# Moving small products, factor sums and a router's preparation in a decoder kernel's attention steps

## The chip, the cores and the metric

The kernel runs on one core of a Trainium2 chip. The metric is the device time of one execution in microseconds (us). The time of the kernel before is the median of three runs.

## The reference

The program is a chain of four layers over tokens of 512 features, each a condition block and a feed-forward block with a residual: `x = x + ffn(cond(x))`. The change touches the third layer (attention, then a feed-forward block with a small router). Cut to what matters:

```python
# attention: 8 sequences x 128 new tokens, 32 query heads, 8 key heads, 512 cached positions
q = rope(rmsnorm(x @ Wq.T));  k = rope(rmsnorm(x @ Wk.T));  v = x @ Wv.T
kc, vc = k_cache[block_table], v_cache[block_table]
k_all, v_all = concat(kc, k), concat(vc, v)            # 640 positions, each key head for 4 query heads
probs = softmax(where(valid, q @ k_all.T * SCALE, -1e30))
cond = (probs @ v_all) @ Wo.T
# feed-forward of the same layer, fed with cond
H = cond @ W.T + b;  z = cond @ A
logits = 0.5 * H[anchors, :8] / scale_H + 0.5 * (z[anchors] @ LiMEs.T) / scale_z
weights = soft_top2(softmax(logits)), repeated for 2 tokens
x = x + H + (z * (weights @ LiMEs)) @ Bmat * scaling
```

Everything is float32. Each step of the chain is computed in full by both kernels.

## The kernel before, in words

The kernel keeps all tokens in on-chip memory. The first two layers come first; then `attention(...)` works in 32 **steps** (`steps`, one for each pair of a group of four query heads with its key head, `qd` of 0 to 7, and a pair of sequences, `p` of 0 to 3). Step n is `qd = n // 4`, `p = n % 4`. In a step there are two halves, j = 0 and 1, one for each sequence of the pair.

The order of the work is written out by hand in `run`: what passes through `kept(...)` stays in program order on its engine. Instructions without it are placed by a scheduler.

What a step n does, with the functions and lines to follow in the code:

- `weigh(n, j)` (L1118, L1122): five score products `st` on TensorE (PE), each followed by an exponential on ScalarE (ACT) into `pT`. `added(n, j)` (L1138): four additions on VectorE (DVE) sum the five blocks of `pT` into `part`.
- `summed(n, j)` (L1146): four small products with ones on PE sum `part` over the partitions. `inverted` (L1153): the reciprocal on DVE. `spread` (L1159, L1161): four copies on DVE and three transfers on the queue of SyncE (SP) give `R` for all partitions; a fourth transfer stores the sums.
- `mix(n, j)` (L1169): five products with the values. `divided` (L1179): `oT` = product times `R`.
- `project(n + 1)`: queries, keys and values of the next step, as seven block products in place of eight (`seven`, L959). The products, in order, are called one, p6 (tile `q_six`), p5 (tile `q_five`), six (tile `q_six` too), and then the second parts of one, p5 and six. Between them stand DVE's additions `u1` (L972), `u2` (L974) and the results (L1008), ACT's copies, and the hooks of the dictionary `at`, which put other work between the products: a hook "c22" runs after the results of the fourth product have been queued.
- `leave(n - 1)`: the output projection of the step before, by the same `seven`, with tiles `wo_one`, `wo_two`, `wo_six`. GpSimd (POOL) makes two of its additions into `y` (L1207, L1202).
- `rotate`, `roots`, `rotated`, `normed`, `turn` prepare the new queries and keys: POOL multiplies by the sines (L1048), DVE by the cosines (L1052: queries' term 128x1024, keys' term 128x256), adds, scales and turns blocks of 32x32 (L1097). SP writes them to memory (`turned_new`, L1090), and `fetch` reads them back in another order (`qT` L1106, `kTn` L1108). Cached keys go the same way (`turn_cached`, L1081, L1086).
- `gather` (L904): POOL collects cached keys and values, eight gathers each.
- `seven` needs sums and differences of its operands' blocks. Those of the tokens are `tokens` (L920), those of the weights `factors()` (L868): four DVE operations for Wq, Wk and Wv of a `qd`, four for Wo. The weights' factors are needed once for each `qd`: those of Wq in the step before its first projection, those of Wo in the step after the first.

`ending(...)` (L1654) holds the feed-forward block of this layer and the fourth layer. It loads six small tensors at once (`small`, L1676, and two more), and clears and loads `b16` (L1690, L1691). Its `prepare` (L1696) turns `A2` with four PE transposes, copies it, multiplies it with `LiT` in four products and copies the result into `WH`. `end.shifted` (L1748) adds a bias to `x` on POOL. In step 30 and 31, `end.turn`, `end.low`, `end.anchors` and `end.product` start the feed-forward block.

On-chip accumulator tiles come from three tags: `st` (three buffers: scores, p6 and the small sums), `mm` (three: one, p5 and six of both projections), `av` (two).

Before the loop, `first(0)` and `first(1)` project and turn steps 0 and 1 while the second layer ends.

## Time and profile before

| what | us |
| --- | --- |
| median of three runs | 1609.87 (1606.64 to 1612.54) |
| the profiled execution | 1615.59 |
| its span, first to last instruction | 1613.7 |
| PE busy / share of the span | 1543.0 / 96% |
| DVE busy | 1078.4 / 67% |
| POOL busy | 850.3 / 53% |
| ACT busy | 537.9 / 33% |
| mean granted TensorE clock | 0.987 |

A row of the profile's timeline gives the start of an instruction (or of several alike, merged), how long it took, the engine (PEld is PE's loading of weights, SPq an issue of SP's queue), the line, the operation, output tile and input tiles, sizes, and in brackets how long the engine stood idle before it and what ended that wait. A row of the waits gives who waited for whom, the total in us, how often, and the longest. A transfer's row is its issue; it lands later.

The steps start, in the profiled execution, where the first `st` product of a step starts: step 0 at 344.75, step 1 at 374.38, step 2 at 407.73, step 31 at 1420.17. Most steps take 33.5 to 35.3 us.

### The profile page before, as it was taken

To read this page: it belongs to the slowest core of one execution; us is meant where nothing else is said; L and a number is where in the kernel's file an instruction comes from. 1 tells how busy PE (TensorE), PEld (TensorE's weight loads), DVE (VectorE), ACT (ScalarE), POOL (GpSimd) and SP (SyncE) were. 2 spreads that over 40 slices of the span, in tenths; PEclk is the share of its full clock that TensorE was granted. 3 is DMA by queue.
4 is the path that set the end of the run, shared out by engine and by line. 5 is a ranking of instruction groups with operands and counts; after the bars stand their busy time and mean duration, and the time that the engine had idled before them with its cause. 6 is when DMAs were issued, how large, how long until landed. Compare 5 with 4: busy or idle time off the path is not lost.

```text
span 1613.7 us, 18969 instructions
## 1 busy us (share of the span) xinstructions
PE 1543.0 (96%) x5985; PEld 925.5 (57%) x5985; DVE 1078.4 (67%) x2123; ACT 537.9 (33%) x1324; POOL 850.3 (53%) x842
## 2 busy tenths in 40 slices
PE   9999998959999999999999999999999999989998
PEld 7888884525555555555555555555555544559653
DVE  4575423466878887787878778777777888843141
ACT  1111110234443444344543434543444444320210
POOL 1341106173766777776777766777757677700000
PEclk9999999979999999999999999999999999999999
DMA  8110003043546444553454444355444435512000
GB/s 293 40 47 24 1 0 98 27 118 83 163 111 185 119 124 120 146 167 102 123 152 122 121 139 139 98 144 158 119 137 114 120 98 144 151 39 71 0 20 35
DMA packets 161358, 169.92 MB, mean 105 GB/s; under 512 B 55713, under 2 KB 128609, under 8 KB 161121
## 3 DMA queue, kind: packets, MB, share of 16 engines
q1 hardware_dynamic: 143104, 131.61, 28.7%
q0 software_dynamic: 17056, 36.49, 7.7%
q8 instruction: 50, 0.82, 0.2%
q10 hardware_dynamic: 1088, 0.52, 0.1%
q14 instruction: 60, 0.48, 0.1%
HBM read 113.89 MB, written 42.07 MB: 97 GB/s over the span
## 4 chain that ended last, share of the span: by engine, by line
PE 70%; DVE 12%; issue 7%; POOL 4%; DMA 4%; SPq 2%; ACT 1%; DVEq 0%; ACTq 0%; POOLq 0%
PE st L1118 11%; PE av L1169 11%; PE g L362 7%; PE q_six L959 5%; PE q_five L959 5%; PE dn L362 4%; PE wo_two L959 4%; DVE part L1138 3%; PE q_one L959 3%; PE wo_six L959 3%; PE wo_one L959 2%; PE z L53 2%; PE h L1672 2%; POOL kn L904 2%; PE o L53 2%
## 5 line engine op out<-in xcount | busy, mean ns | idle before, releaser
L904 POOL DMA_INDIRECT kn<-in_k_cache,kvrow_k x256 | 294.0, 1149 | 75.8 <-issue 67.9
L904 POOL DMA_INDIRECT vals<-in_v_cache,kvrow_v x256 | 261.1, 1020 | 73.6 <-issue 68.6
L1169 PE MATMUL av<-pT,vals 128*128 128x512 f32 x640 | 298.8, 597 | 0.0
L1122 ACT ACTIVATE pT<-st,hide 128x512 f32<-128x512 f32 x256 | 176.0, 688 | 346.4 <-PE av L1169 146.3
L1118 PE MATMUL st<-qT,kT 128*128 128x512 f32 x512 | 241.8, 606 | 10.3 <-DMA qT<-turned_new 8.3
L1048 POOL TENSOR_TENSOR vq<-q,txq 128x256 f32<-128x256 f32 x128 | 120.4, 969 | 198.9 <-ACT sqq L1032 134.9
L1169 PEld LDWEIGHTS av<-pT,vals 128*128 128x128 f32 x640 | 119.1, 190 | 144.5 <-issue 137.8
L1118 PEld LDWEIGHTS st<-qT,kT 128*128 128x128 f32 x512 | 99.0, 194 | 121.7 <-issue 116.1
L1138 DVE TENSOR_TENSOR part<-pT 128x512 f32<-128x512 f32 x128 | 87.4, 685 | 39.9 <-issue 23.7
L1179 DVE TENSOR_TENSOR oT<-av,R 128x512 f32<-128x512 f32 x64 | 44.2, 691 | 85.4 <-DMA R<-R 34.7
L959 PE MATMUL q_one<-q,x 128*128 128x384 f32 x256 | 93.0, 486 | 0.0
L1159 DVE COPY R<-rr 32x128 f32<-32x128 f32 x256 | 84.8, 331 | 3.7
L1032 ACT ACTIVATE sqq<-q 128x128 f32<-128x128 f32 x256 | 79.4, 310 | 11.1 <-DVE q L1008 4.2
L1153 DVE RECIPROCAL rr<-sum 128x128 f32<-128x128 f32 x64 | 60.9, 952 | 23.5 <-PE q_five L959 21.0
L1013 ACT COPY q<-q_one 128x256 f32<-128x256 f32 x32 | 11.9, 372 | 187.4 <-PE q_one L959 180.2
L959 PEld LDWEIGHTS q_one<-q,x 128*128 128x128 f32 x256 | 48.5, 190 | 39.8 <-issue 14.5
L959 PE MATMUL q_six<-q_s,xs_all 128*128 128x384 f32 x192 | 70.0, 487 | 0.0
L959 PE MATMUL wo_one<-o,oT 128*128 128x256 f32 x256 | 65.8, 379 | 0.0
L1118 PE MATMUL st<-qT,kTn 128*128 128x512 f32 x128 | 65.4, 592 | 0.0
L1207 POOL TENSOR_TENSOR y<-y,uo 128x512 f32<-128x512 f32 x32 | 40.9, 1277 | 45.4 <-DVE y L1199 44.9
L959 PE MATMUL wo_two<-o_s,os 128*128 128x256 f32 x256 | 60.5, 379 | 0.0
L362 PE MATMUL g<-xs,ws 128*128 128x256 f32 (+1 forms) x240 | 55.2, 379 | 1.5 <-POOL ws L429 1.5
(394 smaller groups left out, 2729.4 us busy)
## 6 DMA issues: line engine op xcount, KB each, us to landing
turned_new<-qkt SPq DMA_DIRECT2D x128, 160.0 KB
turned_cached<-kt SPq DMA_DIRECT2D x128, 128.0 KB
kT<-turned_cached SPq DMA_DIRECT2D x32, 512.0 KB
qT<-turned_new SPq DMA_DIRECT2D x32, 512.0 KB
R<-R SPq DMA_DIRECT2D x192, 64.0 KB
q<-in_WqT SPq DMA_DIRECT2D x8, 1024.0 KB
o<-in_WoT SPq DMA_DIRECT2D x8, 1024.0 KB
kn<-in_k_cache,kvrow_k POOLq DMA_INDIRECT x256
```

The source lines that it names most:

```text
L53: pe.matmul(o, lhsT, rhs, start=start, stop=stop)
L362: pe.matmul(o, lhsT, rhs, start=start, stop=stop, skip_group_check=True)
L904: kept(pool.indirect_dma_start(out=d[:, c, :], out_offset=None, in_=kc if what == "k" else vc, in_offset=bass.IndirectOffsetOnAxis(ap=kvro ...
L959: kept(pe.matmul(o, l[:, c, :], r[:, c, :], start=start and c == 0, stop=c == 1, skip_group_check=True))
L1032: kept(act.activation(sq, S[n][m][:, j, i, :], AF.Square, accum_out=S[n]["ssq"][:, j, col : col + 1]))
L1048: kept(pool.tensor_tensor(to, t[:, b, :, hi : hi + 64], wx[:, b, lo : lo + 64].unsqueeze(2).to_broadcast(list(to.shape)), ALU.mult,))
L1118: kept(pe.matmul(ps, s["kT"][:, c, 4 * j : 4 * j + 4, :] if c < 4 else s["kn"][:, j], s["qT"][:, :, REP * j : REP * (j + 1), :].rearrange( ...
L1122: kept(act.activation(pT[:, c, :, :].rearrange("p i t -> p (i t)"), ps, AF.Exp, **(dict(bias=hide[:, b, c : c + 1]) if c < 4 else dict(bia ...
L1138: kept(dve.tensor_tensor(o, l, r, ALU.add))
L1153: kept(dve.reciprocal(r, S[n]["sum", j]))
L1159: kept(dve.tensor_copy(R[0:32, i * P : (i + 1) * P], r[32 * i : 32 * i + 32, :]))
L1169: kept(pe.matmul(ps, v[:, c, :], pT[:, c, :, :].rearrange("p i t -> p (i t)"), start=c == 0, stop=c == NC - 1, skip_group_check=True,))
```

## The change

No arithmetic is added or taken away. Work is put elsewhere:

- **Products with ones of the first half.** In the steps that project a next one (1 to 30), `summed(n, 0)`, with `inverted` and `spread`, moves from behind the projection's second product to behind its fourth (hook "c22"). The second half of the output's differences (`outs`) moves behind `u2`.
- **Factors.** Of Wq's four factors, two stay at the end of the step that starts them (n % 4 == 2), one goes among the next step's sums of `pT`, one to hook "u2". Wo's four are spread over "u2", "c22", "c12" and the output projection's "u2". Wo's first factors move from before step 0 into step 1.
- **The keys' cosine term.** `rotate` now returns it as a function, and it is queued behind `u2` of the output projection.
- **The ending.** `ending` is built at the end of step 4 in place of before step 0, with its loads and its memset kept in program order. `prepare` becomes a generator of two parts: the transposes and the first copy come behind the second products with ones of step 5, the products and the copy into `WH` behind that step's last products with the values.
- **Step 0.** Its first products with ones, `fetch(1)`, reciprocal and spread come behind the sums of the second half; `tokens(2)` comes behind the sums of the first half; `divided(0, 0)` comes behind both reciprocals.
- The gather of values of the next step is called before the loads of the ending in step 30. In the order that results, POOL's two additions into `y` stand ahead of that gather in step 30; in all other steps they already did.

```diff
-        end = ending(
-            tc, a, out, x, ident, bias3, experts, late,
...
-        y2 = att.run(late, end, bank, lambda: sp.dma_start(kept, x))
+        def end_of(in_order):
+            return ending(
+                tc, a, out, x, ident, bias3, experts, late,
...
+        y2, end = att.run(late, end_of, bank, lambda: sp.dma_start(kept, x))
@@ rotate
-            kept(dve.tensor_tensor(r, t, ws.unsqueeze(2).to_broadcast(full), ALU.mult))
-            return r, u
+            def straight_terms():
+                kept(dve.tensor_tensor(r, t, ws.unsqueeze(2).to_broadcast(full), ALU.mult))
+
+            S[n]["r" + m] = r, u
+            return straight_terms
...
+        terms("q", S[n]["q"], REP)()
+        return terms("k", S[n]["k"], 1)
@@ run
-        end.prepare(bank)
-        tokens(2)
-        every(WO[0].factors())
-        wo_ops = iter(())
+        end, prepared = None, iter(())
+        w_ops, wo_ops = iter(()), WO[0].factors()
...
             some(outs, 2)()
+            some(w_ops)()
             every(sums_of)
             if after:
                 project(after, {
-                    "six": lambda: summed(n, 0),
-                    "u1": lambda: (some(wo_ops)(), every(outs), inverted(n, 0)),
-                    "u2": lambda: (spread(n, 0), some(wo_ops)()),
+                    "u2": lambda: (every(outs), every(w_ops), some(wo_ops)()),
+                    "c22": lambda: (summed(n, 0), inverted(n, 0), spread(n, 0), some(wo_ops)()),
                     "c11": lambda: (squares(after, "k", 0, (0,)), squares(after, "q", 0, (0, 1))),
-                    "c12": lambda: squares(after, "q", 0, (2, 3)),
+                    "c12": lambda: (squares(after, "q", 0, (2, 3)), some(wo_ops)()),
                 })
-                some(wo_ops)()
-                rotate(after)
+                keys_terms = rotate(after)
...
-                    "u2": lambda: every(wo_ops),
+                    "u2": lambda: (keys_terms(), every(wo_ops)),
...
                 fetch(after)
-            else:
+                gather(after, "v")
+            elif n:
                 summed(n, 0)
                 every(outs)
                 inverted(n, 0)
                 spread(n, 0)
-                if n:
-                    leave(n - 1)
-                else:
-                    fetch(1)
-            if after:
-                if n + 2 == len(steps):
-                    end.load_w2()
-                    end.load_aw()
-                    end.shifted()
-                gather(after, "v")
+                leave(n - 1)
+            else:
+                tokens(2)
+            if n + 2 == len(steps):
+                end.load_w2()
+                end.load_aw()
+                end.shifted()
             mixed = mix(n, 0)
             weigh(n, 1, {2: (some(mixed),), 3: (some(mixed),), 4: (some(mixed, NC),)})
             every(added(n, 1))
-            divided(n, 0)
+            if n == 0:
+                summed(n, 0)
+                fetch(1)
+                inverted(n, 0)
+                spread(n, 0)
+            else:
+                divided(n, 0)
             summed(n, 1)
             inverted(n, 1)
             spread(n, 1)
+            if n == 0:
+                divided(n, 0)
+            if n == 5:
+                prepared = end.prepare(bank, lambda shape, name: wk.tile(shape, F32, tag="xs", name=name, bufs=1))
+            next(prepared, None)
             every(mix(n, 1))
+            next(prepared, None)
...
-                        every(W[steps[n + 2][0]].factors())
+                        w_ops = W[steps[n + 2][0]].factors()
+                        some(w_ops, 2)()
                     tokens(n + 2)
             if n == 3:
                 kept(keep())
+            if n == 4:
+                end = end_of(kept)
@@ ending
-        sp.dma_start(t, src)
+        kept(sp.dma_start(t, src))
...
-    sp.dma_start(WH[:, :, 0:8], chunks(a["W2T"])[:, :, 0:8])
+    kept(sp.dma_start(WH[:, :, 0:8], chunks(a["W2T"])[:, :, 0:8]))
     b16 = early.tile([P, 16], F32, tag="b16", name="b16")
-    pool.memset(b16, 0.0)
-    sp.dma_start(b16[:, 0:8], a["b8"].partition_broadcast(P))
+    kept(pool.memset(b16, 0.0))
+    kept(sp.dma_start(b16[:, 0:8], a["b8"].partition_broadcast(P)))
...
-    def prepare(bank):
+    def prepare(bank, room):
+
         pt = bank("mm", [P, D], "A2Tp")
         for c in range(DC):
-            pe.transpose(pt[:32, c * P : (c + 1) * P], A2[:, c, :], ident)
-        A2T = early.tile([32, D], F32, tag="oT", name="A2T")
-        act.copy(A2T, pt[:32])
+            kept(pe.transpose(pt[:32, c * P : (c + 1) * P], A2[:, c, :], ident))
+        A2T = room([32, D], "A2T")
+        kept(act.copy(A2T, pt[:32]))
+        yield
         ps = bank("mm", [P, DC, 8], "alp")
         for c in range(DC):
-            mm(ps[:, c, :], A2T[:, c * P : (c + 1) * P], LiT, True, True)
-        act.copy(WH[:, :, 8:16], ps)
+            kept(pe.matmul(ps[:, c, :], A2T[:, c * P : (c + 1) * P], LiT, start=True, stop=True))
+        kept(act.copy(WH[:, :, 8:16], ps))
```

## The prediction

> **What bounds the kernel now.** I read first the busy times by engine, and then what TensorE (PE) waited for, longest first.
>
> ```profile
> PE 1543.0 (96%) x5985; PEld 925.5 (57%) x5985; DVE 1078.4 (67%) x2123; ACT 537.9 (33%) x1324; POOL 850.3 (53%) x842
> ...
> PE sum L1146 <- DVE part L1138: 21.2, 19, 5.5
> PE wo_two L959 <- DVE uo L974: 8.5, 9, 2.1
> PE st L1118 <- DMA qT<-turned_new: 8.3, 1, 8.3
> ...
> PE st L1118 <- DMA R<-R: 2.0, 1, 2.0
> ```
>
> PE is busy for 96% of the span, and the change takes no matmul away. All that can be won is PE's idle time, and the slowed matmuls that follow a long idle. Nearly all of it lies in the attention's 32 steps, and the waits name what ends it: the products with ones (L1146) wait for VectorE's sums. So I cut PE's timeline where each step's first score product starts. These are the stretches of steps 0, 3, 4, 7, 13, 28 and 30 (length, then busy time of each engine, then granted clock):
>
> ```profile
> 344.75:374.38 29.63, 23.10 (x56) 9.63 (x57) 16.36 (x30) 6.76 (x10) 15.41 (x15) 0.82 0.48 127
> 441.36:478.80 37.44, 35.06 (x113) 19.18 (x112) 30.21 (x56) 15.06 (x37) 24.16 (x25) 0.95 0.38 102
> 478.80:512.49 33.69, 33.55 (x113) 18.25 (x112) 26.65 (x52) 15.05 (x37) 23.90 (x25) 1.00 0.58 176
> 580.88:615.16 34.28, 33.41 (x113) 18.39 (x112) 28.67 (x52) 15.07 (x37) 24.48 (x25) 1.00 0.41 112
> 785.44:820.70 35.26, 34.02 (x113) 18.11 (x112) 27.91 (x52) 15.05 (x37) 24.97 (x25) 1.00 0.48 139
> 1304.27:1340.37 36.10, 33.67 (x113) 18.29 (x112) 29.87 (x50) 15.05 (x37) 26.62 (x25) 1.00 0.39 106
> 1377.56:1420.17 42.61, 38.49 (x171) 22.18 (x169) 30.96 (x52) 16.23 (x39) 25.39 (x23) 1.00 0.48 141
> ```
>
> Step 1, which waits for nothing, takes 33.35 us with the same 113 groups: that is PE's own time. VectorE is busy 27 to 30 us of such a step, so it can pass as long as its order suits. All times below are counted from a step's start.
>
> **Steps 1 to 31: the products with ones.** Before, they stand behind the projection's second product (PE is there at 7.1 us), and VectorE ends the last sum of pT at 7.14 at best. After, they stand behind the fourth, at 9.5. The wait is then covered for sums up to 2.3 us late. I sum by kinds of step.
>
> Even steps 2, 4 to 26 (13 of them): 437.95 us together, to 33.35 each, -4.4. Steps 7, 11, 15, 19, 23: VectorE makes four factors of Wq (0.95 each) at the end of the step before, and the sums come 0.9 late. After, two of the four lie there and two among the sums; parts end at 8.0 and cover holds. 171.4 to 166.8, -4.7. Steps 3 and 27 have token combinations besides (four of 0.42), and the wait is 2.4 to 2.9, after which PE runs slow:
>
> ```profile
> 450.77 0.47 PE L1146 MATMUL sum<-part,ones 128*32 128x128 f32 x8 [2.38 <-DVE part L1138]
> 451.17 2.93 PE L959 MATMUL q_five<-q_s,xs_all 128*128 128x384 f32 x4
> ```
>
> After, oT starts at 3.4 in place of 5.1 and the sums are ready by 8.7: 75.3 to 67.0, -8.3.
>
> Steps 9, 13, 17, 21 make the four factors of Wo (0.69 each, 1.25 beside a GpSimd product). They lose at three places: sum, q_six, and wo_two, which waits for the add L974 behind the two rotary terms. After, u2's add no longer stands behind the reciprocal, and k's term (0.95) is moved behind L974. Adding the starts of the queue's instructions in the new order from 7.14, I get L974 done at 17.9, where PE wants it at 18.2. But VectorE's work is the same, so the turned queries (L1097) come at 22.4 in place of 23.1 to 23.7. From there to the next step's first product pass 11.3 us in the mean (write, fetch, completion; from 10.7 to 11.9 by step), and these steps have 0 to 0.8 us of slack there now: the queries' fetch becomes the bound, at 33.9. 140.9 to 135.6, -5.3. Step 25 is of this kind (36.22 to 34.1, -2.1), step 29 too, with its sums 1.1 later (37.19 to 34.5, -2.7). Step 1 becomes such a step, since Wo's first factors move into it: 33.35 to 33.95, +0.6. Step 5 gets the ending's router: four transposes (0.60) and eight small products (1.05) on PE, less what overlaps: 34.71 to 34.8, +0.1. Its second part (the copy into WH) is 0.19 on ScalarE in step 6's beginning, where ScalarE has 7.6 us idle. The six loads move on SP's queue to step 5, between kT (9.8) and R (12.8): 6 x 0.42 = 2.5, which just fits; the memset of 0.13 lies in GpSimd's gap.
>
> **Steps 28 and 30: a stall that only shrinks.**
>
> ```profile
> 1319.41 4.58 POOL L1748 TENSOR_TENSOR x<-x,bcol 128x2048 f32<-128x2048 f32 x1
> ...
> 1320.45 3.82 DVE L1052 TENSOR_TENSOR r<-k,tsk 128x256 f32<-128x256 f32 x1
> 1324.19 0.41 DVE L972 TENSOR_TENSOR uo<-wo_two,uo 128x256 f32<-128x256 f32 x1
> ```
>
> k's term takes 3.82 in place of 0.95 and PE waits 2.1 behind it. By the rows alone, moving it behind the adds frees PE: -2.7 at step 28. The Trainium skill (SBUF — State Buffer, Who interferes with whom) speaks against that: a VectorE instruction with two SBUF inputs and a GpSimd one that reads SBUF exclude each other for the whole instruction, whichever came second waits; with one input from PSUM there is no clash. The trace agrees: the adds from PSUM take 0.42 beside GpSimd. So k's term still waits for the end of GpSimd's addition, now at 19.3, and y's first add stands behind it, which the last product (wanted at 19.1) waits for until 20.2. Step 28 goes to 34.8, -1.3, and I take that; step 30 likewise, -1.1. In 30 GpSimd's two additions into y move ahead of the gather of values, away from the copies of R (L1159 took 2.00 there instead of 0.22). SP issues the last queries' fetch behind two transfers of R, so it goes out about 2 us sooner, and with the idle of 2.16 goes the half clock at step 31's head. Of some 5 I take -4.5 for 30 and 31, because y's additions now meet the sums of pT.
>
> **Step 0: the fetch of the first queries.**
>
> ```profile
> 328.45 1.50 DVE L1097 STREAM_TRANSPOSE qkt<-r 128x1280 f32<-128x1280 f32 x1
> ...
> 334.99 0.13 POOL L1690 MEMSET b<- 128x16 f32 x1
> ...
> 335.15 0.34 SPq L1691 DMA_DIRECT2D b<-in_b  x1
> 335.60 1.95 SPq L1090 DMA_DIRECT2D turned_new<-qkt  x4
> ...
> 340.24 0.65 SPq L1106 DMA_DIRECT2D qT<-turned_new  x1
> 344.75 5.60 PE L1118 MATMUL st<-qT,kT 128*128 128x512 f32 x8 [8.31 <-DMA qT<-turned_new]
> ```
>
> The turned queries are there at 329.95, but SP writes them at 335.60: its queue stands at the load of b, which waits for a memset behind GpSimd's gathers. With the ending moved, the write goes out at 330.0, the fetch at 334.6 (4.64 later, as now), the first product at 339.2 (4.51 later). Then PE has 40 records of 0.43 = 17.2, 0.7 of products with ones, 2.1 of half clock at the start as now, and one wait: it is at the second products with ones at 354.6. VectorE's queue sets their inputs: L1097 of step 1 ends at 349.8 (it waits for a landing that the change leaves alone), then four sums, four token combinations (1.45) and four sums (2.8 each four): 356.9, so 2.3 idle. Step 1 starts at 361.7. A rule makes it later: the clock falls after an idle window, and the windows of about 3.4 us run free (the Trainium skill, TensorE: Matmul & The Clock Gate, What's actually happening). The rows cannot say for 2.3: 2.38 idle was followed by half clock in step 3, 2.11 in step 28 was not. The rows alone give 361.7, the rule up to 363.4; I take 362.9 against 374.4, -11.5. Step 1's own fetch, now ahead of R, lands at about 359.5 and is covered.
>
> **The sum**, on the profiled execution (1615.59, of it 1613.7 span): -11.5 +0.6 -4.4 -4.7 -8.3 -5.3 +0.1 -2.1 -2.7 -1.3 -4.5 = -44.1. The stalls set at nothing can only come out above it, so I take -42: 1573.6 for such an execution. The profiled one lies 5.7 above the median, so the median is 1609.87 - 42 = 1568.
>
> **Rivals.**
> *The reciprocal waits for a late completion.* In step 4 it starts 2.77 us after the products with ones and only "until q_five"; in step 7 after 1.00. Sixteen even and Wo steps show the long form. If it keeps it behind the fourth product, the reciprocal starts at 12.2 in place of 10.3, and the rest of the queue, the queries' fetch included, slides by 1 to 1.7: even steps +0.15, Wq steps +0.2, seven Wo steps +1.5. Sum +14: 1580. For it: the two steps with no wait before these products, 25 and 30, show it. Against: in step 1, with none either, and at all second halves but one it is prompt.
> *Step 0 gives little.* If the earlier write crosses the gathers of keys (GpSimd issues them until 335) or PE then stands longer at the sums, its gain is 3 to 5: 1575.
> *GpSimd's addition overtakes.* In step 28 the query term started 0.14 us before it. If it starts after, it is blocked for 3.5 and PE for about 3, twice, and the clock falls: +9, 1577.
> *The change doesn't do what it says: the late queue goes on to the next wait.* If VectorE is the true limit of all steps, the waits reappear at wo_two and at the fetch, and only step 0, 3, 27, 30 and 31 gain: 1586.
> *Slower.* Everything from the reciprocal on is moved behind the fourth product's two adds. If that brings the turned queries later than 23.5 in even and Wq steps (21.3 now; slack in the fetch 0.7 less the 0.3 that the step is shorter), each of 28 steps pays beyond that. From 1.6 us per step on it takes all back; at 2, 1620. Nothing shows 2.2 us of such delay: the late completion accounts for 0.9.
>
> **How the numbers follow.** As summed 0.51; late completion 0.24; step 0 small 0.08; overtaking 0.05; VectorE's limit 0.06; slower 0.04; no change 0.02. About 0.3% (5 us) is what a measurement can tell from none. Ends of the unknown: step 0 at best -12.7, Wo steps at 33.5, 28 and 30 as the rows alone have them, in all -53: 1556. Late completion with half of step 0 lost, -44 +14 +6: 1586. So 1556 to 1588; the likeliest case alone 1558 to 1576. Faster 0.94, same 0.02, slower 0.04.
>
> **What would show it.** SP's write of turned_new at about 330 and the first score product near 339; no wait of sum on part except in steps 0 and 31; even steps of 33.35; wo_two's wait on uo small, a new one of wo_six on y in 28 and 30; Wo steps at 33.9 with st waiting for qT. Wrong if the reciprocal idles until q_five's end, if wo_two waits for q_five's bank, or if L1097 starts after 22.5 in even steps.

## The result, and the profile after

The median went from 1611.2 us (four runs, 1606.6 to 1616.5) to 1589.7 (four runs, 1588.6 to 1592.5): 0.9868 of the time before, 95% interval 0.9834 to 0.9902, or 21.5 us. The forecast was 1568, with 1556 to 1588. The sign was right, the size half of what was forecast, and the result lies 1.7 us outside the range. The profiled executions went from 1615.6 to 1588.6, 27.0 us. One run among all of the study was slow, over 1.5% above the fastest of its kernel (the profiled one of `b_undo_factors2`, 1609.9); it is left out of the medians below and not read.

The busy times of the kernel after, and what its TensorE waited for (total, times, longest):

```profile
PE 1536.3 (97%) x5985; PEld 925.2 (58%) x5985; DVE 1088.0 (69%) x2123; ACT 537.8 (34%) x1324; POOL 849.9 (54%) x842
```

```profile
PE sum L1152 <- DVE part L1144: 9.1, 4, 5.1
...
PE wo_six L962 <- DVE y L1205: 5.2, 10, 0.8
PE st L1124 <- DMA kTn<-turned_new: 4.9, 1, 4.9
...
PE st L1124 <- DMA qT<-turned_new: 2.0, 3, 1.2
...
PE hd L53 <- issue: 1.0, 1, 1.0
...
PE wo_two L962 <- DVE vals L1011: 0.7, 1, 0.7
```

The wait of the products with ones (`sum`, now L1152) fell from 21.2 us in 19 places to 9.1 in 4, as the change set out to do. Two things are new: the last output product `wo_six` waits in ten steps for `y` (L1205), and 5.1 us of the rest stand in one place, step 0. The same stretches as before (steps 0, 3, 4, 7, 13, 28, 30), in the kernel after:

```profile
339.49:368.01 28.52, 23.40 (x56) 9.83 (x57) 17.54 (x31) 6.87 (x10) 17.88 (x18) 0.78 0.50 133
435.29:469.89 34.60, 33.99 (x113) 18.06 (x112) 30.72 (x55) 14.95 (x37) 23.96 (x24) 1.00 0.41 111
469.89:503.31 33.42, 33.42 (x112) 18.47 (x113) 26.89 (x53) 15.06 (x37) 23.99 (x26) 1.00 0.58 177
572.13:605.48 33.35, 33.35 (x113) 18.30 (x112) 28.82 (x50) 14.96 (x37) 23.07 (x24) 1.00 0.42 115
773.46:807.45 33.99, 33.61 (x114) 18.31 (x113) 27.58 (x49) 15.06 (x37) 23.18 (x23) 1.00 0.50 141
1279.15:1315.12 35.97, 33.85 (x114) 18.12 (x112) 27.96 (x53) 15.05 (x37) 28.65 (x26) 1.00 0.42 109
1350.09:1392.50 42.41, 38.57 (x170) 22.14 (x169) 29.47 (x53) 16.23 (x39) 26.87 (x24) 1.00 0.50 145
```

Steps 3, 4 and 7 came down to about the floor of 33.35. Steps 28 and 30 hardly moved, and step 0 got 1.1 us shorter where 6 were forecast. Every step cut in this way gives the account below. The last column is an execution of the same changed kernel in the last group of runs (group 5 of the experiments).

| part | before | forecast | after | after, last group |
| --- | --- | --- | --- | --- |
| first product of step 0 | 344.8 | 339.2 | 339.5 | 340.5 |
| start of step 1 | 374.4 | 362.9 | 368.0 | 365.5 |
| step 1 | 33.35 | 33.95 | 33.94 | 33.93 |
| 13 even steps | 438.0 | 433.6 | 433.8 | 433.6 |
| steps 7, 11, 15, 19, 23 | 171.4 | 166.8 | 166.7 | 166.7 |
| steps 3 + 27 | 75.3 | 67.0 | 68.9 | 66.7 |
| steps 9, 13, 17, 21 | 140.9 | 135.6 | 137.3 | 135.8 |
| step 5 | 34.7 | 34.8 | 35.4 | 35.4 |
| steps 25 + 29 | 73.4 | 68.6 | 70.1 | 68.9 |
| step 28 | 36.1 | 34.8 | 36.0 | 36.1 |
| step 30 to the end | 236.2 | 231.7 | 236.7 | 233.4 |
| span | 1613.7 | 1569.6 | 1586.7 | 1575.9 |

Against the sum of -44.1, 17.1 us are missing: 5.1 up to step 1, 5.0 from step 30 on, 1.9 in steps 3 and 27, 1.7 in the four Wo steps, 1.5 in 25 and 29, 1.2 in 28, and the rest in small amounts.

**Step 0.** VectorE and TensorE of the kernel after (in brackets the idle time ahead and what ended it; `remote` is an end that the profile could not trace to an instruction):

```profile
352.71 0.69 DVE L1144 TENSOR_TENSOR part<-part,pT 128x512 f32<-128x512 f32 x1
...
354.45 0.42 DVE L923 TENSOR_TENSOR xs<-x,xs 128x256 f32<-128x256 f32 x1
358.08 1.29 DVE L1144 TENSOR_TENSOR part<-pT 128x512 f32<-128x512 f32 x2 [3.21 <-remote]
...
355.40 0.43 PE L1152 MATMUL sum<-part,ones 128*32 128x128 f32 x8
360.95 0.65 PE L1152 MATMUL sum<-part,ones 128*32 128x128 f32 x8 [5.12 <-DVE part L1144]
```

The forecast let VectorE go from the token combinations (`xs`, done at 354.87) straight to the second half's sums. It stands idle for 3.21 us instead. `part` has one buffer in the program, and the second half may not be written into it until the first products with ones have read it. Those were moved behind the last of the first half's products with the values and run at 355.40 to 355.83. VectorE starts only at 358.08, which is 2.2 us later still: it saw the end of the products late. Such **late ends** come back below.

**Steps 28 and 30.** GpSimd (POOL), VectorE and TensorE in step 28, and then in step 30:

```profile
1293.90 4.58 POOL L1766 TENSOR_TENSOR x<-x,bcol 128x2048 f32<-128x2048 f32 x1
...
1296.68 2.08 DVE L1056 TENSOR_TENSOR r<-k,tsk 128x256 f32<-128x256 f32 x1
1298.69 0.41 DVE L1205 TENSOR_TENSOR y<-wo_six,y 128x256 f32<-128x256 f32 x1
1300.07 1.46 DVE L1068 TENSOR_TENSOR r<-r,vq 128x1024 f32<-128x1024 f32 x1 [0.97 <-POOL vq L1051]
...
1315.12 1.13 PE L1124 MATMUL st<-qT,kT 128*128 128x512 f32 x2 [1.23 <-DMA qT<-turned_new]
...
1377.23 1.65 POOL L1213 TENSOR_TENSOR y<-y,uo 128x512 f32<-128x512 f32 x1 [4.44 <-DVE y L1205]
1377.07 2.35 DVE L1144 TENSOR_TENSOR part<-pT 128x512 f32<-128x512 f32 x2
1381.41 0.43 PE L1152 MATMUL sum<-part,ones 128*32 128x128 f32 x8 [1.59 <-DVE part L1144]
```

The keys' term (L1056) ends with GpSimd's addition, as forecast from the Trainium skill (SBUF — State Buffer, Who interferes with whom): 1298.76 against 1298.48, 2.08 us in place of 0.95. What the forecast left out stands one row on: two of GpSimd's own four products `vq` are queued behind the same addition, so the rotated queries come late (0.97 idle), and the next step's first score waits 1.23 for their fetch. In step 30 the two additions into `y`, moved ahead of the gathers, fall on the sums of pT: two sums take 2.35 in place of 1.27 (step 28), and the second products with ones wait 1.59.

### The profile page after: what moved, and what is told of

It is laid out like the page before. It is cut to its first block, busy times and chain, and to the rows that moved or that the text cites. A ratio compares the mean times of both kernels' runs of the same rounds, so it can differ in the third digit from the quotient of the medians.

```text
span 1586.7 us, 18970 instructions
## 1 busy us (share of the span) xinstructions
PE 1536.3 (97%) x5985; PEld 925.2 (58%) x5985; DVE 1088.0 (69%) x2123; ACT 537.8 (34%) x1324; POOL 849.9 (54%) x842
## 4 chain that ended last, share of the span: by engine, by line
PE 83%; DVE 6%; POOL 4%; DMA 3%; issue 3%; ACT 1%; SPq 1%; another core or an unknown queue 0%; ACTq 0%; DVEq 0%; POOLq 0%
PE st L1124 16%; PE av L1175 16%; PE g L362 7%; PE q_six L962 7%; PE q_one L962 5%; PE q_five L962 5%; PE dn L362 5%; PE wo_two L962 4%; PE wo_six L962 3%; PE wo_one L962 3%; PE z L53 2%; PE h L1688 2%; PE o L53 2%; PE sum L1152 2%; PE eo_l L53 1%
## 5 line engine op out<-in xcount | busy, mean ns | idle before, releaser
L907 POOL DMA_INDIRECT kn<-in_k_cache,kvrow_k x256 | 280.6, 1096 | 75.7 <-issue 66.9
L907 POOL DMA_INDIRECT vals<-in_v_cache,kvrow_v x256 | 255.2, 997 | 73.6 <-issue 57.8
L1051 POOL TENSOR_TENSOR vq<-q,txq 128x256 f32<-128x256 f32 x128 | 125.5, 1010 | 173.2 <-DVE q L1011 156.7
L1165 DVE COPY R<-rr 32x128 f32<-32x128 f32 x256 | 104.5, 408 | 4.7
L962 PE MATMUL q_one<-q,x 128*128 128x384 f32 x256 | 96.2, 498 | 0.0
L1128 ACT ACTIVATE pT<-st,rs 128x512 f32<-128x512 f32 x64 | 44.0, 687 | 38.4 <-PE st L1124 20.4
```

The source lines that it names most:

```text
L907: kept(pool.indirect_dma_start(out=d[:, c, :], out_offset=None, in_=kc if what == "k" else vc, in_offset=bass.IndirectOffsetOnAxis(ap=kvro ...
L962: kept(pe.matmul(o, l[:, c, :], r[:, c, :], start=start and c == 0, stop=c == 1, skip_group_check=True))
L1051: kept(pool.tensor_tensor(to, t[:, b, :, hi : hi + 64], wx[:, b, lo : lo + 64].unsqueeze(2).to_broadcast(list(to.shape)), ALU.mult,))
L1128: kept(act.activation(pT[:, c, :, :].rearrange("p i t -> p (i t)"), ps, AF.Exp, **(dict(bias=hide[:, b, c : c + 1]) if c < 4 else dict(bia ...
L1165: kept(dve.tensor_copy(R[0:32, i * P : (i + 1) * P], r[32 * i : 32 * i + 32, :]))
```

## The experiments

The kernels were run in five groups. The kernels of a group ran side by side on one chip, with runs of the kernel before among them, so times are given as ratios to those. Medians of different groups are not to be compared directly. "After" is the changed kernel; `after_again`, `after_third`, `after_fourth` and `after_fifth` are the same kernel run again.

| group (before) | kernel | median us | ratio, 95% interval |
| --- | --- | --- | --- |
| 1 (1607.1) | a_sums: sums moved alone | 1586.0 | 0.9868 [0.9836, 0.9900] |
| 1 | a_ending: ending moved alone | 1608.4 | 1.0006 [0.9991, 1.0020] |
| 1 | b_undo_sums: after, sums back | 1590.1 | 0.9887 [0.9855, 0.9920] |
| 1 | b_undo_factors: after, factors back | 1577.6 | 0.9828 [0.9786, 0.9870] |
| 2 (1610.1) | after_again | 1587.8 | 0.9866 [0.9848, 0.9883] |
| 2 | before_again (one run) | 1617.5 | |
| 2 | c_step0 (one run) | 1592.6 | |
| 2 | c_all | 1581.6 | 0.9815 [0.9798, 0.9833] |
| 3 (1613.7) | after_third | 1595.1 | 0.9896 [0.9872, 0.9920] |
| 3 | b_undo_factors2 | 1593.6 | 0.9877 [0.9844, 0.9909] |
| 3 | c_keys_shift | 1585.1 | 0.9827 [0.9804, 0.9850] |
| 3 | c_all2 | 1583.2 | 0.9819 [0.9795, 0.9842] |
| 4 (1608.1) | after_fourth | 1589.3 | 0.9878 [0.9852, 0.9903] |
| 4 | after_gather | 1586.5 | 0.9860 [0.9839, 0.9881] |
| 4 | c_gather | 1578.4 | 0.9812 [0.9790, 0.9835] |
| 5 (1605.6) | after_fifth | 1577.8 | 0.9818 [0.9793, 0.9843] |
| 5 | a_sums2: sums moved alone | 1586.5 | 0.9872 [0.9849, 0.9896] |

### One part of the change alone

`a_sums` is the kernel before with only the first half's products with ones moved:

```diff
-                    "six": lambda: summed(n, 0),
-                    "u1": lambda: (some(wo_ops)(), every(outs), inverted(n, 0)),
-                    "u2": lambda: (spread(n, 0), some(wo_ops)()),
+                    "u1": lambda: some(wo_ops)(),
+                    "u2": lambda: (every(outs), some(wo_ops)()),
+                    "c22": lambda: (summed(n, 0), inverted(n, 0), spread(n, 0)),
```

> The kernel before with one part of the change alone: the first half's products with ones, reciprocal and spread behind the projection's fourth product, the output's differences behind u2. Theory (the sums are late by less than two products take): the wait of sum on part goes from steps 2 to 29; the even steps come to 33.35 us (-4.4 together), steps 7, 11, 15, 19, 23 to 33.4 (-4.7), steps 3 and 27 to 34.5 (-6), steps 9, 13, 17, 21 hardly change (35.0, their wait goes on to wo_two), step 0 keeps its 29.6 and its start at 344.7; in all -15 to -17. Rival (VectorE's queue is the limit and its lateness goes on to the next wait): the Wq steps and steps 3 and 27 keep two thirds of their loss as waits of q_six and wo_two; in all -7.

Measured: even steps 433.6 together, the five Wq steps 166.7, steps 3 + 27 66.7, the four Wo steps 136.8 (137.5 in `a_ending` beside it, which has the order of before in them); step 0 starts at 342.8 and takes 27.6. The theory holds and was too careful: 21 us by the medians. This one edit makes the even steps, the Wq steps and steps 3 and 27 (with the token combinations) what they are after the change.

`a_ending` is the kernel before with only `ending` built behind step 4 and prepared in step 5.

> The kernel before with the ending alone built behind step 4 and prepared in step 5; the order of step 0 and everything else as before. Theory A (what the prediction assumed: step 0's start carries through to step 1's): first score product at 339.5 in place of 344.75 and step 1 starts 5 us or more sooner, at 369 or below. Theory B (VectorE's queue, which stands until 348 to 349 at the turning of step 1's queries, sets the first half's sums): the first score product comes at 339.5 all the same, but the first products with ones stay at 356.7 and step 1 starts at 373.5 to 374.5; gain 0 to 1 us in all.

Measured: ratio 1.0006, the first score product at 339.83, step 1 at 373.20. Theory B. TensorE and VectorE in step 0 of this kernel:

```profile
339.83 1.70 PE L1121 MATMUL st<-qT,kT 128*128 128x512 f32 x3 [3.83 <-DMA kTn<-turned_new]
...
353.68 0.68 DVE L871 TENSOR_TENSOR o_s<-o,o_s 128x512 f32<-128x512 f32 x1
...
357.28 0.65 PE L1149 MATMUL sum<-part,ones 128*32 128x128 f32 x8 [11.22 <-DVE part L1141]
```

Five microseconds were won at the start of step 0 and nearly all were lost at the next wait, which grew from 5.5 to 11.2: VectorE goes through the turned queries, the token combinations and four factors before it reaches the sums. So the sooner fetch is worth nothing by the median without the new order of step 0 behind it.

### One part of the change undone

`b_undo_sums` puts the first half's products with ones back behind the second product, and `b_undo_factors` puts the weights' factors back where they stood (second diff):

```diff
+                    "six": lambda: summed(n, 0),
+                    "u1": lambda: (every(outs), inverted(n, 0)),
-                    "u2": lambda: (every(outs), every(w_ops), some(wo_ops)()),
+                    "u2": lambda: (every(w_ops), spread(n, 0), some(wo_ops)()),
-                    "c22": lambda: (summed(n, 0), inverted(n, 0), spread(n, 0), some(wo_ops)()),
+                    "c22": lambda: some(wo_ops)(),
```

```diff
-            some(w_ops)()
-                    "u2": lambda: (every(outs), every(w_ops), some(wo_ops)()),
-                    "c22": lambda: (summed(n, 0), inverted(n, 0), spread(n, 0), some(wo_ops)()),
+                    "u1": some(wo_ops),
+                    "u2": lambda: (every(outs), some(wo_ops)()),
+                    "c22": lambda: (summed(n, 0), inverted(n, 0), spread(n, 0)),
-                    "c12": lambda: (squares(after, "q", 0, (2, 3)), some(wo_ops)()),
+                    "c12": lambda: squares(after, "q", 0, (2, 3)),
-                        some(w_ops, 2)()
+                        every(W[steps[n + 2][0]].factors())
```

> The changed kernel with the first half's products with ones back behind the projection's second product, the reciprocal at u1 and the spread at u2, the factors still spread. Theory: the wait of sum on part returns in the even steps (33.7 each, +4.4), in 7, 11, 15, 19, 23 (34.3 each, +4.7) and in 3 and 27 (+5), in all +14 to +17 over the changed kernel. Rival (the spread factors alone would have freed VectorE in time): +5.

> The changed kernel with the weights' factors where they stood before: Wq's four at the end of the step, Wo's at u1, u2, behind the projection and at the output projection's u2. Theory (cover of two products, 2.3 us): the Wq steps stay at 33.4 (their sums come 0.9 late, which is covered), steps 3 and 27 lose 1 each, the Wo steps stay within 0.5 of 34.3; in all +1 to +4. Rival (the spreading is what made room): waits of sum on part return in 7, 11, 15, 19, 23 with 0.5 or more, in all +8.

Measured: `b_undo_sums` lies 12.5 us above its neighbour `b_undo_factors`, by the ratios 9.5. The loss does not lie where either side put it: the even steps take 445.8 in place of 433.6 (+12.2; +4.4 was expected), the Wq steps 167.8 (+1.0; 34.3 each was expected), steps 3 + 27 69.5 (+2.8; +5 was expected), and the Wo steps are shorter, 134.4. So the moved sums count most in the even steps. In the Wq steps and in 3 and 27 the change without them still does much of what they do alone: in the order of before (`a_ending`, same group) these take 171.6 and 73.6. Without the moved sums the kernel is still 17.0 us below the kernel before, so the gains of the parts do not add up.

With the factors put back, all Wq steps stay at 33.35 and the Wo steps at 33.94. The median, 1577.6, was 12 us below the 1589.7 of the changed kernel, where 1 to 4 above (or 8 above, by the rival) was expected. That comparison was between groups, and the next ones showed that it misleads.

### The same kernels once more, side by side

> The kernel before once more, profiled beside the other experiments. Theory (the execution shown first was a slow one of its kind): the span comes out near the run with the ending alone, whose steps have the same order (1604 to 1609), with steps 3 and 27 together at 73.6 (75.3 in the execution shown) and steps 9, 13, 17, 21 at 137.5 (140.9). Rival: it repeats 75.3 and 140.9, and the ending's move is what shortened them.

Measured, in one run: span 1615.7, the Wo steps 141.0 again, as the rival has it; steps 3 + 27 at 73.3, as the theory has it. So the profiled execution of before shown first was no accident; but in group 1 the same order of steps (`a_ending`) had given 137.5.

> The changed kernel once more, profiled and timed beside the other experiments. Theory (the spread factors themselves cost time): steps 9, 13, 17, 21 again at 136.5 to 137.5 and steps 3 and 27 at 68.5 or more, where the kernel with the factors put back has 135.8 and 66.7; median 1584 to 1590, slower than that kernel's 1577.6. Rival (the execution shown was unlucky): it reads like the kernel with the factors put back, 1576 to 1580.

Measured: 1587.8, Wo steps 137.1, steps 3 + 27 67.6 (68.5 or more was expected). It reads like the result shown first. That the spread factors are the reason is not shown by this; the next pair tests it.

> The changed kernel a third time, as the first rung of a ladder whose four kernels are run side by side: changed kernel, factors put back, two more edits in the steps, step 0 mended. Theory: about 22 us under the kernel before (ratio 0.986 to 0.988), step 0 at 25 to 29 and steps 9, 13, 17, 21 at 135 to 137.

> The changed kernel with the weights' factors put back where they stood, beside the changed kernel. Theory (the earlier gap of 10 us between the two is mostly that they were not run side by side; step by step the factors' spreading costs 0.5 in steps 9 to 21, 0.7 to 2 in 3 and 27): 2 to 4 us under the changed kernel. Rival (spreading costs what the medians said): 8 us or more under it. Second rival (spreading helps, as it was costed at -5.3 with its cover): above the changed kernel.

Measured: 1595.1, with a step 0 of 32.0 and Wo steps of 138.6, both above what was expected; and 1593.6 for `b_undo_factors2`, whose runs spread from 1583.9 to 1598.7. The difference of 1.5 us is below the theory's 2 to 4 and small against that spread: no worth of the factors' spreading can be told either way. So the 10 us between groups 1 and 2 was not the factors. It is a difference between groups, and the profile shows one: how long VectorE's reciprocal stands idle for the products with ones. Kernel before, kernel after (both as shown first), and `a_sums2` of group 5:

```profile
DVE rr L1153 <- PE q_five L959: 21.0, 16, 1.6
```

```profile
DVE rr L1159 <- PE sum L1152: 2.5, 9, 0.5
```

```profile
DVE rr L1153 <- PE sum L1146: 0.9, 1, 0.9
```

In groups 1 and 5 this idle time is at most 0.9 us in the whole execution of every kernel, the order of before (`a_ending`) included. In the executions shown first and in groups 2 to 4 it is 2 to 18, and 20 to 23 in the order of before. In the execution of before shown first the reciprocal stands idle 1.5 to 1.6 us in each of twelve steps, with the products with ones over; in the changed kernel mostly 0.3 to 0.5 in a step, and longer in step 0. It is not the chip alone: by the record groups 4 and 5 ran on the same chip (number 2), about nine minutes apart.

### Mending step 0

`c_step0` starts from the kernel with the factors put back; the second half's sums of step 0 get a tile of their own, and the token combinations go behind them:

```diff
+        if (n, j) == (0, 1):
+            both = late[0].tile([P, 4, 2, P], F32, tag="os", name="parts_0_1").rearrange("p a b t -> p (a b t)")
+            t, u = both[:, 0 : REP * P], both[:, REP * P :]
...
-            else:
-                tokens(2)
...
             if n == 0:
+                tokens(2)
                 summed(n, 0)
```

> The changed kernel with the factors put back where they stood, and step 0 mended: the sums of its second half go into a tile of their own, and the four token combinations come behind them. Theory (the second products with ones wait because VectorE may not write the second half's sums until the first half's products have read the buffer): their wait of 3.2 us or more falls to 0.5 or less, and the half clock behind it goes; step 0 takes 20.5 to 22.0 in place of 25.2. Rival (VectorE's queue behind the turned queries is late by itself): the wait stays above 2, step 0 above 24.

Measured: step 0 takes 20.84, as the theory says: the shared buffer made most of the wait (the edit also takes the four token combinations, 1.45 us by the prediction, from ahead of these sums). But step 1 took 41.7 in place of 33.9. TensorE stops 1.9 us into it for 4.8 us. By the trace it is released there by the second reciprocal, which comes 10 us behind the products that it reads and holds a bank that the scores need.

`c_all` adds two edits, which `c_keys_shift` below has alone, and `c_all2` gives step 0's products with ones a bank that the scores do not use:

```diff
-        S[n]["sum", j] = ps = psa.tile([P, P], F32, tag="st", name=f"sum_{n}_{j}", bufs=3)
+        S[n]["sum", j] = ps = psa.tile([P, P], F32, tag="st" if n else "mm", name=f"sum_{n}_{j}", bufs=3)
```

> As the kernel with step 0 mended, and two edits more: the keys' cosine term behind the output projection's first result in place of ahead of it, and the bias of the ending added to x on ScalarE in step 31 (eight operations) in place of GpSimd in steps 28 and 30. Theory: the wait of wo_six on y goes everywhere (0.5 in steps 1, 5, 9, 13, 17, 21, 25, 29 and 0.95 in 28 and 30), step 28 comes to 33.4 (36.1), step 30 to 39 (40.8), the Wo steps to 33.4; 1562 to 1566. Rival (the queries' fetch is the bound behind it): the Wo steps keep 33.8 with a wait of st for qT, and step 30 keeps its wait of sum; 1570 to 1573.

> As the third rung, with step 0 mended: its second half's sums in a tile of their own, the token combinations behind them, and step 0's products with ones in a bank that the scores do not use. Theory A (the stall in step 1 came from the score's bank, held until the second reciprocal): step 0 at 20.8 and step 1 at 33.4, 7 us under the third rung. Theory B (TensorE's results are seen late there whatever the bank): step 0 at 20.8, step 1 at 38 or more, within 2 us of the third rung.

Measured: `c_all` 20.7 and 40.4 for steps 0 and 1, `c_all2` 21.0 and 41.0. By the medians, 1581.6 and 1583.2. Both expectations for `c_all` miss (1562 to 1566, 1570 to 1573): step 28 comes to 33.35 and step 30 to 39.7, but step 1 stays at 40.4, and the four Wo steps take 139.1. `c_all2` lies 1.9 below `c_keys_shift` (the third rung). Theory B: the stall stays without the shared bank, so the bank is not the reason. TensorE, VectorE and GpSimd there:

```profile
354.03 0.40 PE L1156 MATMUL sum<-parts,ones 128*32 128x128 f32 x8
...
362.01 0.96 DVE L1163 RECIPROCAL rr<-sum 128x128 f32<-128x128 f32 x1 [7.08 <-PE st L1124]
...
364.88 0.96 DVE L1163 RECIPROCAL rr<-sum 128x128 f32<-128x128 f32 x1 [0.98 <-remote]
365.88 1.22 PE L1124 MATMUL st<-qT,kT 128*128 128x512 f32 x1 [4.38 <-ACT pT L1128]
...
361.28 0.94 POOL L907 DMA_INDIRECT vals<-in_v_cache,kvrow_v  x1 [0.30 <-issue]
```

The products with ones are over by 354.5, and VectorE, with nothing else to do from 354.9 on, sees the end of the first at 362.0. Even ScalarE's exponentials of step 1 come late, the first at 365.1 for a score that ended at 359.8. What ends near 362 is GpSimd's train of gathers, whose last one is issued at 361.28; the second reciprocal and ScalarE come 2.7 us or more behind it.

The trace also notes when an engine's semaphore counts (the counter by which the others learn that a piece of its work is done). Of `c_all2`'s TensorE, ten counted pieces end between 354.2 and 361.5; ten counts are noted, one at 361.99 and nine in one burst from 364.86 to 365.20. So it was the counts that came late, and not VectorE that was slow to take them up.

### What holds the ends back

`after_gather` is the changed kernel with the eight gathers of step 1's values kept until step 0's second reciprocal is done; `c_gather` is `c_all2` with the same edit:

```diff
         first(1)
-        gather(1, "v")
...
+                r = S[0]["r", 1][:, 0:1]
+                kept(pool.tensor_tensor(late[0].tile([P, 1], F32, tag="hold", name="hold"), r, r, ALU.add))
+                gather(1, "v")
```

> The changed kernel beside the two others of this group. Both theories: step 0 at 28 to 35 us if this chip shows the late ends of the products with ones (25.2 to 25.8 if it does not, and then the group tells nothing of them), ratio to the kernel before 0.986 to 0.990.

> The changed kernel with one edit: the eight gathers of step 1's values wait for step 0's second reciprocal (GpSimd reads one column of it first). Theory (while GpSimd issues gathers, the ends of TensorE's products with ones are seen late): VectorE begins the second half's sums at once after the first products with ones, the wait of sum on part falls from 5 us or more to 3.0 (what the shared buffer costs), step 0 takes 25.2 to 26 and step 1 stays at 33.9; 3 us or more under the changed kernel. Rival (the lateness has nothing to do with the gathers): step 0 stays at 28 to 35.

> The mended kernel (factors put back, keys' term behind the first result, ScalarE's bias, step 0's second sums in their own tile, sums in a bank that the scores do not use) with the same edit to the gathers. Theory (gathers hold the ends back): step 0 at 20.8, step 1 at 33.4 to 34 in place of 41.0, and 6 to 8 us less than without the edit: ratio to the kernel before 0.977 to 0.979. Rival: step 1 stays at 40 to 41, ratio 0.982.

Measured, side by side: the changed kernel's step 0 takes 28.5 with a wait of 5.8, and with the gathers held back 25.8 with 3.0. `after_gather`, TensorE, VectorE and GpSimd:

```profile
353.87 0.43 PE L1152 MATMUL sum<-part,ones 128*32 128x128 f32 x8
354.43 1.29 DVE L1144 TENSOR_TENSOR part<-pT 128x512 f32<-128x512 f32 x2 [1.99 <-PE sum L1152]
...
357.30 0.55 PE L1152 MATMUL sum<-part,ones 128*32 128x128 f32 x8 [3.00 <-DVE part L1144]
...
360.19 0.23 POOL L1328 TENSOR_TENSOR hold<-rr 128x1 f32<-128x1 f32 x1 [7.94 <-DVE rr L1159]
```

VectorE now starts 0.13 us behind the first products with ones. In `c_gather`, both reciprocals follow as soon as VectorE is free:

```profile
357.28 0.43 PE L1156 MATMUL sum<-parts,ones 128*32 128x128 f32 x8
357.63 4.56 PE L1179 MATMUL av<-pT,vals 128*128 128x512 f32 x10
...
358.51 0.95 DVE L1163 RECIPROCAL rr<-sum 128x128 f32<-128x128 f32 x1
...
360.51 0.96 DVE L1163 RECIPROCAL rr<-sum 128x128 f32<-128x128 f32 x1
...
361.55 0.23 POOL L1331 TENSOR_TENSOR hold<-rr 128x1 f32<-128x1 f32 x1 [6.33 <-DVE rr L1163]
```

Step 0 takes 21.1 and step 1 35.9 (41.0 without the edit; 33.4 to 34 was expected, and 1.2 went to new waits of q_five, q_six and wo_six). So the theory holds in step 0: with the gathers out of the way, the ends of TensorE's products are seen at once. In `c_gather` the train moves to 361.9 to 371.8, and a late end with it: VectorE takes up `q_five`, over at 370.35, at 373.59, though it is free from 372.0.

```profile
368.90 1.45 PE L962 MATMUL q_five<-q_s,xs 128*128 128x384 f32 x4
...
373.59 0.56 DVE L977 TENSOR_TENSOR uq<-q_five,uq 128x384 f32<-128x384 f32 x1 [1.57 <-PE q_one L962]
```

Could the two executions with the edit simply be of the kind that has no late ends, as in groups 1 and 5? Their traces say no. Of TensorE's counts that fall due from step 0 to step 30 while a train of gathers runs, 41% have no note within 0.12 us in `after_gather` and 45% in `c_gather`. In the two executions shown first and in all others of groups 2 to 4 it is 38 to 47%, and 8 to 15% outside of the trains; in groups 1 and 5 it is at most 0.7% in a train and none outside. Whether a count without a note came late or was only not noted, the trace does not say. The edit moves GpSimd's issuing and the transfers that it starts together; which of the two holds the ends back is not shown.

By the medians the edit to the changed kernel is worth 2.7 us (3 or more was expected), with intervals that overlap. `c_gather` lies 10.9 us below the changed kernel beside it and has the lowest ratio of the study, though five others, the changed kernel in group 5 among them, lie within its interval. The ratio, 0.981, is above the expected 0.977 to 0.979: against `c_all2`'s 0.982 in another group, the 5 us of step 1 are not seen in the whole.

### Keys' term, and the bias of the ending

`c_keys_shift` is the kernel with the factors put back and two edits:

```diff
-                    "u2": lambda: (keys_terms(), every(wo_ops)),
-                    "c22": lambda: (rotated(after), normed(after), turn(after)),
+                    "u2": lambda: every(wo_ops),
+                    "c22": lambda: (keys_terms(), rotated(after), normed(after), turn(after)),
...
-            pool.tensor_tensor(
-                x[:, :, half(g)], x[:, :, half(g)], bcol.unsqueeze(2).to_broadcast([P, DC, 512]), ALU.add
-            )
+            for c in range(DC):
+                kept(act.activation(
+                    x[:, c, half(g)], x[:, c, half(g)], AF.Identity, bias=bcol[:, c : c + 1], scale=1.0
+                ))
```

> The kernel with the factors put back, and two edits: the keys' cosine term behind the output projection's first result in place of ahead of it, and the ending's bias added to x by ScalarE in step 31 in place of GpSimd in steps 28 and 30. Theory: the wait of wo_six on y goes (0.5 in eight steps), step 28 comes from 36 to 33.4 and step 30 from 41 to 39; 6 to 9 us under the kernel with the factors put back. Rival (queries' fetch and VectorE's queue are next in line): the Wo steps stay at 33.9 or more, step 30 stays; 2 to 4 us.

Measured: 8.5 us below the kernel beside it, as the theory said. Step 28 comes to 33.35 exactly, here and in the three kernels that add to these edits (`c_all`, `c_all2`, `c_gather`). The two edits were not tried apart; the rows of step 28 above say that GpSimd's addition held both the keys' term and the fetch. Step 30 comes to 40.6 (39.7, 39.4 and 39.2 in the three), from 44.0 in `after_third`; but the changed kernel has 40.8 there in group 5 without the edits, so how much of it is theirs is not shown. The Wo steps are at 136.1, 34.0 each, as the rival has it: wo_six still waits 0.15 to 0.23 in some of them. That the fetch is next is seen behind one of the four only (the first score waits 0.31 behind step 21).

### The sums alone, beside the whole change

> The changed kernel beside the kernel with the products with ones moved alone. Theory (the rest of the change gains in step 0 what it gives back in the steps with Wo's factors): ratio 0.986 to 0.990 and within 4 us of the other. Rival (step 0 and the ending are worth what was forecast, 11 us): 8 us or more under it.

> The kernel before with the products with ones moved alone, beside the changed kernel. Theory: ratio 0.986 to 0.990, within 4 us of the changed kernel, with step 1 starting 2 to 6 us later than there and steps 9, 13, 17, 21 no longer than there. Rival: ratio 0.993 or more, 8 us or more above it.

Measured: 1577.8 and 1586.5. The rival: the rest of the change is worth 8.7 us here. Step 1 starts at 365.5 in place of 372.8 (-7.3), and step 30 takes 40.8 in place of 42.5. This group shows no late ends, and the changed kernel gains 27.8 us in it. What the rest is worth where ends are late was not measured side by side. Steps 0, 3, 13, 28 and 30 of the changed kernel there:

```profile
340.46:365.51 25.05, 22.04 (x57) 9.37 (x57) 16.87 (x31) 6.87 (x10) 17.32 (x17) 0.84 0.53 146
432.79:466.13 33.34, 33.34 (x113) 18.39 (x112) 28.60 (x55) 15.05 (x37) 23.28 (x24) 1.00 0.40 111
768.97:802.90 33.93, 33.61 (x114) 18.30 (x113) 27.59 (x49) 15.05 (x37) 23.59 (x23) 1.00 0.49 140
1271.55:1307.60 36.05, 33.85 (x114) 18.12 (x112) 27.93 (x53) 15.05 (x37) 28.67 (x26) 1.00 0.42 111
1342.51:1383.30 40.79, 38.40 (x170) 22.11 (x169) 29.47 (x53) 16.22 (x39) 26.89 (x24) 1.00 0.53 149
```

Step 3 is at the floor, and every Wo step takes 33.93 to 33.98: the up to 1.2 us more that single steps of the execution shown first took are absent. Step 0 still waits 3.0:

```profile
355.90 0.43 PE L1152 MATMUL sum<-part,ones 128*32 128x128 f32 x8
356.46 1.29 DVE L1144 TENSOR_TENSOR part<-pT 128x512 f32<-128x512 f32 x2 [1.64 <-PE sum L1152]
...
359.33 0.66 PE L1152 MATMUL sum<-part,ones 128*32 128x128 f32 x8 [3.01 <-DVE part L1144]
359.92 5.75 PE L1175 MATMUL av<-pT,vals 128*128 128x512 f32 x10
```

VectorE starts 0.13 behind the first products with ones here; 1.64 us of idle are the shared buffer's. Behind the wait the last five products with the values take 5.75 us, where they take 4.56 in step 0 of `c_gather`.

## Why the prediction was right or wrong

**Steps 1 to 27: right in the main.** Even steps, Wq steps and step 1 came within 0.2 us of their terms in both executions of the changed kernel in the table, and the sums alone produce the even and the Wq steps. Steps 3 and 27 and the Wo steps came within 0.3 us of their terms where ends are prompt (66.7 for 67.0, 135.8 for 135.6), and 1.9 and 1.7 above them in the execution shown. Step 5 came 0.6 above its term in both. The Wo term had the right size for a wrong reason: the step said that the queries' fetch would be the bound at 33.9, but what waits is wo_six on y (0.5), behind the keys' term and the last factor, where the prediction looked for that wait only in 28 and 30. In these steps moving the keys' term behind the adds moved the wait one product on.

**Step 0: mis-sized, -11.5 forecast and -6.4 measured (-8.9 in the last group), two causes.** The write and the first score came where they were forecast (339.5 for 339.2). The step that failed is "then four sums, four token combinations and four sums": it counted VectorE's durations and not the buffer. The first products with ones were put behind the last product with values of the first half, and the second half's sums must wait for them: in the last group TensorE waits 3.0 us where 2.3 were forecast, and VectorE stands idle 1.64 for the buffer. On top of it came the late end of those products, which nothing in the prediction costed for step 0: 2.2 us in the execution shown, 3.0 in group 4, 5.3 in group 3. In the execution shown the wait is 5.1, 2.8 over its term. The rule that the clock falls after an idle window (the Trainium skill, TensorE: Matmul & The Clock Gate, What's actually happening) would have cost up to 1.7 us and was taken at 1.2. The trace has the fall, also behind an idle of 3.0, which is shorter than the page's window of about 3.4. From the second products with ones to step 1 pass 6.2 us behind the wait of 3.0 in the last group and 7.1 behind that of 5.1 in the execution shown, where `c_gather`, which does not wait, takes 4.75; so it cost 1.4 and 2.3. The granted clock over the step was 0.84 and 0.78. The rest is a slower start: 0.3 us later and 0.8 us more for the first scores in the execution shown, 1.3 and 0.4 in the last group. And the edit that was credited with the gain, the ending out of SP's way, is worth 0 alone.

**Steps 28 and 30 to the end: mis-sized.** -1.3 and -4.5 were forecast, -0.1 and +0.5 came (-0.1 and -2.8 in the last group). In 28 the keys' term and wo_six behaved as forecast (wo_six waits 0.8), but the step named only what stands behind the keys' term on VectorE. GpSimd's own queue was not followed: two of its four products for the queries stand behind the addition, and the fetch became the bound. In 30 the meeting of y's additions with the sums of pT was seen and guessed at half a microsecond; it costs a wait of 1.6, in both executions. The half clock at the head of step 31 stayed in the execution shown, behind new idle time of `hd`, and went in the last group, where that idle is absent.

**From the profile to the median.** The sum was made on an execution of 1615.6 and taken off a median of 1609.9. Executions fell by 27.0, medians by 21.5. The profile of before lay 4.4 above its median of four and the profile of after 1.1 below its own. A constant distance between the two was assumed and not shown; this is 5.5 of the 21.7 us by which the forecast missed. The rest is 17.1 of the sum, less the 2.1 already taken back for stalls set at nothing, and 1.3 by which the median of before rose with its fourth run.

**Rivals.** "The reciprocal waits for a late completion" named the right phenomenon and the wrong place: behind the fourth product it shrank to 2.5 us of idle. There GpSimd's gathers are over (in steps 2 to 15 of the execution shown the last one ends 0.15 us or more before the products). It came out in step 0, where they go on. "Step 0 gives little" (1575) and "the late queue goes on to the next wait" (1586) each happened in part. The overtaking and the slower case did not happen.

**What stays open.** Why groups 1 and 5 see the ends at once, with the same gathers, is not shown. Nor is every end in a train late: in the kernel before, the five Wq steps have a gather in the same place as the even steps (issued 0.15 us before the products with ones end), and their reciprocals start 0.57 us behind the products, those of twelve even steps 2.1 to 2.4. That late ends lengthen the Wo steps and steps 3 and 27 in the other groups is argued from the step lengths; only in step 0 was it tried.

## What to carry to other kernels

When an instruction is moved, follow its buffers as well as its queue: a sum that is read later also keeps its tile later, and the next half cannot be written. When an operation on one engine blocks another, follow both queues behind it. A single edit that ends a long wait early may be worth nothing until the next wait's own queue is short, and a gain is safest taken from one part alone, beside the whole, on the same chip.

## What the runs showed of the hardware that was not expected

- In step 0, while GpSimd issued a train of gathers (0.94 to 1.3 us each), the ends of TensorE's products were seen 2 to 8 us late by VectorE, and in `c_all2` by ScalarE too; with the gathers held back, 0.1 us. In groups 1 and 5 the same trains did no harm.
- The traces tell the two kinds of execution apart: of TensorE's counts due in a train of gathers, 38 to 47% have no note within 0.12 us in the executions with late ends, and at most 0.7% in the others.
- In the order of before, late ends show in half of the steps: in the execution shown 16 reciprocals stand idle for 21.0 us in all, where `a_ending` has one of 0.9.
- The changed kernel differs from group to group by more than its runs inside one (at most 9.3 us apart): its medians were 1587.8, 1595.1, 1589.3 and 1577.8, the last two with the same chip number. Those of the kernel before, 1605.6 to 1613.7, differ by less than its runs inside a group.
